# Reordering the query units of a fused four-layer kernel, and joining two heads' score tiles

## The chip, the cores and the metric

The kernel runs on one core of one Trainium2 chip. It is one program with one launch; the metric is the time of the program in microseconds (us), the median of several executions. Its engines are TensorE (PE, with its weight loads as PEld), VectorE (DVE), ScalarE (ACT), GpSimd (POOL) and SyncE (SP), which issues the DMAs. Each engine works through its own instructions in the order in which the program gives them, and waits at semaphores for the others.

## The reference

Input x has 2048 tokens of 128 features. Four layers follow each other, each an attention and a feed-forward part, both on a layer norm of the stream, in float32:

```python
x = x + L0_attn(layernorm(x))   # 16 heads of 8, full softmax over 2048 keys
x = x + L0_ffn(layernorm(x))    # 128 -> 512 -> 128, exact gelu
x = x + L1_attn(layernorm(x))   # 16 heads of 64, full softmax over 2048 keys
x = x + L1_ffn(layernorm(x))    # gated, integer weights / 127
x = x + L2_attn(layernorm(x))   # 16 heads of 8, each token sees its two neighbours, i-1 and i+1 modulo 2048
x = x + L2_ffn(layernorm(x))    # 8 experts, top 1
x = x + L3_attn(layernorm(x))   # a recurrence: 32 chunks of 64 tokens, each needs the state after the chunk before
x = x + L3_ffn(layernorm(x))    # 8 experts, top 2, and a shared one
```

Two things in it matter here. The second layer's attention (L1) is the bulk of the work. And in the third layer's attention (L2), token 0 needs token 2047: so the first block of the layers behind L1 attention needs the last token's L1 output, and each block needs the first token of the next.

## The kernel before

The stream stays on chip as `xs`, 128 x 16 x 128. The program has three stages. **The first** is layer 0, with the keys and values of layer 1 as they become ready; they go to DRAM (`kvd`, `khd`). **The second** is L1 attention (`l1_attn`, line 1066). **The third**, called the tail here, is what is left of the layers behind it, after the last score.

L1 attention runs over 40 *units*. A unit is one query block times one pair of heads (`units`, line 373). The five blocks stand in `QB` (line 33) as first token, number of tokens, and columns computed: 512, 384, 512, 384 and 256 tokens. The second block has 388 columns: its 384 own tokens and places for the *edge tokens* 1280, 1792 and 2047 (`EXTRA`), whose L1 output is computed early so that the neighbour attention of the layer behind needn't wait for their blocks. `stage_m` takes these few tokens alone through the L1 feed-forward part and makes the neighbours' keys and values; nothing of the neighbour attention starts before it (`s_b`, line 1959).

A unit has 16 *steps*, one for each 128 keys. In a step, for both heads of the pair:

- PE makes the scores, transposed (keys in the partitions), in four passes into two banks of the three in the pool `st`: high by high part, low by high, high by low, and the row of negated maxima (`ops`).
- ACT takes the exponentials into `P`, one tile of 128 x 512 for each head, from a pool of seven.
- PE makes a share of the *maxima products* for a later unit (`u_max`, `max_upto`): queries by keys into a bank of the pool `mx`, which DVE reduces to a row maximum (`mx<-mi` in the profile). The pool `mx` has five banks; the accumulator of the values and all banks of the other work come from it too.
- The tile of the step before is multiplied with the values (`do_pv`) and added to the sum of exponentials (`do_sum`, line 1099): by POOL into `acg` at steps 0 to 13, by DVE into `acd` at steps 14 and 15 (`dve` in `T`). The first tile of each sum is only noted, so POOL has 13 additions a head and DVE one; at the unit's end DVE adds `acg` to `acd` (`do_merge`).

`u_end` then makes the column sums, their reciprocals by way of DRAM, and the product `o<-o,rb` on DVE; `stage_wo` projects and adds to `xs`.

**What sets the order.** All instructions are put in order by hand in Python: the functions of all layers behind attention are generators in `parts` and `helpers`, and a planner with a clock for each engine (`note`, `clk`, `COST`) steps whichever piece is ready by its estimate. `fill` (line 246) is called between the exponentials and the products with the values; it steps pieces until PE's estimated clock has moved on by a limit. With `only="t"` it takes pieces alone that need no new bank and hold no product (`Part.may`, line 202). `fill` never changes what a piece does, only where it stands in each engine's queue.

Behind attention, blocks of 256 tokens go through `stage_a` and `stage_a2` (L1 feed-forward, and keys and values of the neighbours), `stage_b`, `stage_b2` (neighbour attention, top-1 experts), `stage_c` (inputs of the recurrence, 128 tokens at a time), `chunk` (32 of them in a chain), `stage_d`, `stage_g` (router of the last layer), `stage_e0` (starts the bank `ac` that sums the experts' outputs) and `s_lane`: 13 tiles of expert weights a block, spread over two lanes, and over seven in the tail, loaded from DRAM. In the built program the first block's `stage_e0` stands in unit 38, and no expert product before the tail.

Of the kernel before, what the change touches and what calls it, by code (L numbers as in the profile page):

```python
# [20 lines left out]
D = 128  # L21
# [10 lines left out]
T = dict(lead0=22, more0=4, mgap=0.4, pvq=2, lim0=0.5, fq=(3,), pl=-0.5, pr=1.0, tlow=2, tback=3, late=0.3, pvp="mx", mxp="mx", ex=(1280, 1792, 2047), low=1, lows='ge', keep=1, leave=2, pvn=1, sp=0, rdy=40., eu=2, qg=(22, 16, 10), em=2, el=6, sem=0.2, same=1.2, tsame=3.0, order="hdmBbAaEcCeg", ps=dict(st=3, mx=5), dma=2.3, slack=0.1, lim=0.3, backlog=2.5, lead=(10, 8, 6), pp=7, dve=(14, 15), qp=(1, 1), lanes=2, xl=5,  # L32
         QB=[(0, 512, 512), (512, 384, 388), (896, 512, 512), (1408, 384, 384), (1792, 256, 256)])

# [36 lines left out]
def body(ctx: ExitStack, tc: tile.TileContext, x, pa, pb, pc, pi, pd, pr, pr0, pe, pw, out):  # L71
# [90 lines left out]
    pp = ctx.enter_context(tc.tile_pool(name="pp", bufs=T["pp"]))  # L162
# [31 lines left out]
    class Part:  # L194
# [24 lines left out]
        def step(self):  # L219
            piece[0] = clk["T"]  # L220
            r = next(self.gen, "end")
            self.same = r == "same"
            self.ready = 0.0 if self.same else piece[0] + (r if type(r) is float else 0.0)
            self.pe = r == "T"
            self.banks = r if type(r) is int else 0
            self.seen = len(emitted) if r is False else -1
            if r == "end":
                emitted.add(self.key)
            return r != "end"
# [140 lines left out]

    QB = T["QB"]
    EXTRA = T['ex']
    units = [(qb, p) for qb in range(len(QB)) for p in range(NP1)]
    qhh, qfs, kmx, mx1 = {}, {}, {}, {}

    qx = [mid.tile([128, 8], F32R, name=f"qx{i}") for i in range(2)]
    xq = {}

    def u_loadx(qb):
        t0, tn, n = QB[qb]  # L380
        xq[qb] = l1x.tile([128, 512], F32, name="xq", tag="xq", bufs=2)
        if n != tn:
            ge.memset(xq[qb][:, tn:n], 0.0)
            for i, t in enumerate(EXTRA):
                sy.dma_start(xq[qb][:, tn + i:tn + i + 1], xnd[:, t:t + 1])
        sy.dma_start(xq[qb][:, :tn], xnd[:, t0:t0 + tn])

    def u_qprep(u):
        qb, p = units[u]
        if qb not in xq:  # L390
            u_loadx(qb)
# [3 lines left out]
        mm(ps[:, :n], C("wq", p * 128, 128), xq[qb][:, :n])  # L395
# [10 lines left out]
        if n > tn:  # L406
            for e in range(2):
                r = slice(64 * e, 64 * e + 64)
                se.copy(qx[u % 2][r, 4 * e:4 * e + n - tn], qf[r, tn:n])
# [15 lines left out]
    def u_max(u, i):  # L425
# [8 lines left out]
        if 128 * qt == tn:  # L434
            ps = amx()
            mm(ps[0:8], qx[u % 2], kmx[(u, c)])
            ve.tensor_reduce(mx1[u][0:8, 0, 3, c:c + 1], ps[0:8], AX.X, ALU.max)
# [11 lines left out]
    def u_maxend(u):  # L449
# [6 lines left out]
        if n > tn:  # L456
            ve.tensor_reduce(m[0:8, 0, 3:4], mx[0:8, 0, 3, :], AX.X, ALU.max)
        yield 1
        t = mi()
        if n > tn:  # L460
            te.transpose(t[0:1, 256:264], m[0:8, 0, 3:4], ident[0:8, 0:8])
# [5 lines left out]
        if n > tn:  # L467
            for e in range(2):
                se.mul(mbt[u % 2][64 * e:64 * e + 1, tn:n], t[0:1, 256 + 4 * e:256 + 4 * e + n - tn], -1.0)
# [50 lines left out]
    l0w = l0ctx.enter_context(tc.tile_pool(name="l0w", bufs=2))  # L520
    qd = dram.tile([16, 6, 8, S], BF16, name="qd")
# [150 lines left out]
    def l0_attn():  # L672
# [49 lines left out]
        for g in range(N):  # L722
# [9 lines left out]
            for q in range(4):  # L732
# [17 lines left out]
                p = pp.tile([128, 512], F32, name="P", tag="P")  # L750
# [202 lines left out]
    leave[0] = T["leave"]  # L953
# [10 lines left out]
    l1a = ctx.enter_context(tc.tile_pool(name="l1a", bufs=2, reuse_waits="tile"))  # L964
# [11 lines left out]
    def u_end(u, o, accs):  # L976
# [4 lines left out]
        if u == len(units) - 1:  # L981
            for e in range(2):
                mm(t[64 * e:64 * e + 64, :n], ones[:, 0:64], accs[e][:, :n], par=(e == 1))
# [8 lines left out]
        for e in range(2):  # L992
            mm(t[32 * e:32 * e + 32, :n], ones[:, 0:32], accs[e][:, :n], tile_position=(0, 32 * e), par=(e == 1))
# [29 lines left out]
    def stage_wo(qb, part):  # L1023
# [4 lines left out]
        for p in range(2 * part, 2 * part + 2):  # L1028
            mm(ps[:, :n], C("wo", p * 128, 128), O.pop(p)[:, :n], start=(p % 2 == 0), stop=(p % 2 == 1))
            yield  # L1030
        if part == 0:
            w = l1w.tile([128, 512], F32, name="wac", tag="wac", bufs=1)
# [9 lines left out]
        del wacc[qb]  # L1042
        yield 1
# [9 lines left out]
        if n != tn:  # L1053
            ne = len(EXTRA)
            xm = edge_x[0] = sm.tile([ne, 128], F32, name="xm", tag="xm", bufs=1)
            for i, t in enumerate(EXTRA):
                sy.dma_start(xm[i:i + 1, :], xs[t % 128:t % 128 + 1, t // 128, :])
# [8 lines left out]
    def l1_attn():  # L1066
        LEAD = dict(zip((256, 384, 512), T["lead"]))
        LEAD.update({260: LEAD[384], 388: LEAD[512]})
# [13 lines left out]
        def do_pv(g, pts, v):  # L1082
            u, k = divmod(g, 16)
            n = QB[units[u][0]][2]
            if k == 0:
                pv[u] = take([T["pvp"]])
            for e in range(2):
                mm(pv[u][64 * e:64 * e + 64, :n], v[:, k % SPC, 64 * e:64 * e + 64], pts[e][:, :n],
                   start=(k == 0), stop=(k == 15), par=(e == 1))
            if k == 15:  # L1090
# [5 lines left out]
                rel(pv.pop(u))  # L1096
                ends.append((u, o, accs))

        def do_sum(g, pts, v):
            u, k = divmod(g, 16)  # L1100
            n = QB[units[u][0]][2]
            for e in range(2):
                a = acc.setdefault(u, [None, None])
                f = first.setdefault((u, e), {})
                eng, nm = (ve, "d") if k in T["dve"] else (ge, "g")
                if nm not in f:
                    f[nm] = [pts[e]]
                    continue
                if len(f[nm]) == 1:
                    if u:  # L1110
                        need(("s", u - 1), ("o", u - 1))
                    t = l1a.tile([128, 512], F32, name="ac" + nm, tag="ac" + nm)
                    eng.tensor_tensor(t[:, :n], f[nm][0][:, :n], pts[e][:, :n], ALU.add)
                    f[nm] = [t, 1]
                else:
                    t = f[nm][0]
                    eng.tensor_tensor(t[:, :n], t[:, :n], pts[e][:, :n], ALU.add)
                if k == 15:
                    a[e] = f["d"][0]
                    merge.append((f["d"][0], f["g"][0], n))  # L1120
                    del first[(u, e)]
# [3 lines left out]
        def do_merge():  # L1125
            while merge:
                d, g_, n = merge.pop(0)
                ve.tensor_tensor(d[:, :n], d[:, :n], g_[:, :n], ALU.add)
            while ends:
                u, o, accs = ends.pop(0)  # L1130
                helper(("o", u), u_end(u, o, accs), max(wr[tname(t)] for t in accs))
# [4 lines left out]
        for g in range(16 * U):  # L1136
# [6 lines left out]
            if u + 2 < U:  # L1143
                if k == 1 and units[u + 2][1] == 0:
                    need(("q", u + 1))
                    u_loadx(units[u + 2][0])
# [10 lines left out]
            pts = []  # L1157
# [3 lines left out]
            for i, (a, b) in enumerate(ops):  # L1161
                for e in range(2):
                    rows = slice(64 * e, 64 * e + 64)
                    mm(pss[e][:, :n], a[rows], b[rows, :n], start=(i == 0), stop=(i == 3), par=e and 0.02)
            for e in range(2):
                pt = pp.tile([128, 512], F32, name="P", tag="P")
                se.activation(pt[:, :n], pss[e][:, :n], AF.Exp)
                rel(pss[e])
                pts.append(pt)
            max_upto(max_at(g + 16 + LEAD[n] + 1))  # L1170
            fill()
            if prev:
                do_sum(*prev[-1])
            if len(prev) == T["pvn"]:
                while prev:
                    do_pv(*prev.pop(0))
                fill()
            do_merge()
# [135 lines left out]
    def stage_m():  # L1314
# [22 lines left out]
        xt = sm.tile([128, 4], F32, name="xtm", tag="xtm", bufs=2)  # L1337
        yield from norm_T(xt)
        h = sm.tile([128, 12], F32, name="hm", tag="hm", bufs=1)
        for k in range(3):  # L1340
# [4 lines left out]
            th = sm.tile([128, 4], F32, name="thm", tag="thm", bufs=2)  # L1345
# [3 lines left out]
            ve.scalar_tensor_tensor(h[:, 4 * k:4 * k + ne], th[:, :ne], 0.5, ps[:, 64:64 + ne], ALU.mult, ALU.mult)  # L1349
# [3 lines left out]
        for k in range(3):  # L1353
            mm(ps[:ne, :128], h[:, 4 * k:4 * k + ne], tok(wi, 6 + k), start=(k == 0), stop=(k == 2))
# [763 lines left out]
```

## Time and profile before

| | |
|---|---|
| median of 3 runs | 2989.47 us (2988.46 to 3006.5) |
| the profiled execution | 3001.08 us, span 2999.2 us |
| first layer, to the first score of L1 | 0 to 906 us |
| L1 attention | 906 to 2596 us |
| tail | 2596 to 2999 us |
| PE / DVE / ACT / POOL busy | 2769.9 / 2194.9 / 1582.9 / 1522.3 us |
| POOL's additions `acg<-acg,P`, 960 of them | 1011.4 us, 1083 ns each |
| DVE's reductions `mx<-mi`, 2080 of them | 1322.1 us, 683 ns each |

A line of the table by stretches has the stretch, its length, the busy time and the number of instructions of PE, PEld (its weight loads), DVE, ACT and POOL, the granted share of PE's clock, the share of the DMA engines and GB/s. A wait line has who waited for whom, the total in us, the number of times, and the longest. A line of the timeline has start and duration in us, engine, line, operation, output and input tile, and shape. Nearly all instructions show one source line, 147, that of the helper through which they are issued; the tiles' names tell them apart. PE's records are modelled at their ends, so a busy PE includes some overlap.

### The profile page before, as it was taken

Reading aid. Unit: us, or ns where it says so; the run is one execution under the profiler, and the core shown is the slowest. Engines: PE = TensorE matmul, PEld = TensorE weight load, DVE = VectorE, ACT = ScalarE, POOL = GpSimd, SP = SyncE. Lnnn points to the kernel's source line nnn. Section 1 sums busy time; section 2 is a strip of 40 time slices with the busy share of each in tenths; the row PEclk is TensorE's granted clock in tenths of the full one; section 3 lists DMA queues with packets and bytes.
Section 4 is the critical chain, followed back from the end, with each engine's and each line's share of the span. In section 5 each row is a group of like instructions: output and inputs, shape, how many; then the busy total and the mean of one; then the engine's idle time right before and its main releaser. Section 6 shows DMA issues by size and latency. Waiting matters only on the chain.

```text
span 2999.2 us, 49776 instructions
## 1 busy us (share of the span) xinstructions
PE 2769.9 (92%) x16719; PEld 1307.0 (44%) x16719; DVE 2194.9 (73%) x4699; ACT 1582.9 (53%) x3933; POOL 1522.3 (51%) x1762
## 2 busy tenths in 40 slices
PE   7999999999979899999999999899989898888998
PEld 2222222322234344454444444455544555565666
DVE  7899898898534666566666778887677769787765
ACT  1788887888854444444444444444434334333444
POOL 2400110201127688866776876677767556443444
PEclk9999999999979999999999999999999999776779
DMA  6311231321144333433442332233334343312244
GB/s 142 72 28 22 72 84 17 101 54 46 53 141 135 92 112 110 121 110 111 138 119 87 94 95 87 89 105 108 109 97 114 108 117 94 88 52 61 76 104 115
DMA packets 247749, 275.80 MB, mean 92 GB/s; under 512 B 95747, under 2 KB 183330, under 8 KB 247366
## 3 DMA queue, kind: packets, MB, share of 16 engines
q1 hardware_dynamic: 246630, 272.43, 33.2%
q8 instruction: 132, 2.16, 0.3%
q14 instruction: 123, 1.01, 0.1%
q10 hardware_dynamic: 864, 0.20, 0.0%
HBM read 229.97 MB, written 42.28 MB: 91 GB/s over the span
## 4 chain that ended last, share of the span: by engine, by line
PE 70%; DVE 18%; ACT 6%; issue 3%; DMA 3%; POOL 1%; SPq 0%; ACTq 0%; DVEq 0%; POOLq 0%
PE mi L147 70%; DVE mx L147 5%; ACT P L147 3%; DVE sB L147 1%; DVE o L147 1%; DVE gq L147 1%; DMA ka<-kvd 1%; DVE gt L147 1%; DVE xs L147 1%; ACT kf L147 1%; ACT kh L147 1%; DVE xn L147 1%; DVE sG L147 1%; DVE acd L147 1%; DVE sA L147 0%
## 5 line engine op out<-in xcount | busy, mean ns | idle before, releaser
L147 DVE TENSOR_REDUCE mx<-mi 128x1 f32<-128x512 f32 (+1 forms) x2080 | 1322.1, 683 | 582.8 <-PE mi L147 571.5
L147 ACT ACTIVATE P<-mi 128x512 f32<-128x512 f32 (+3 forms) x2304 | 1137.0, 551 | 1004.1 <-PE mi L147 973.2
L147 POOL TENSOR_TENSOR acg<-acg,P 128x512 f32<-128x512 f32 (+3 forms) x960 | 1011.4, 1083 | 181.8 <-ACT P L147 180.0
L147 PE MATMUL mi<-P,ka 128*64 128x512 f32 (+3 forms) x2560 | 597.6, 546 | 2.3 <-DVE mx L147 2.3
L147 PE MATMUL mi<-qh,ka 64*128 64x512 f32 (+3 forms) x2560 | 521.0, 406 | 9.7 <-DMA ka<-kvd 6.8
L147 PEld LDWEIGHTS mi<-qh,ka 64*128 64x128 f32 x2560 | 247.0, 189 | 382.5 <-issue 347.0
L147 PE MATMUL mi<-kop,qop 48*128 48x512 bf16 x1024 | 348.6, 405 | 24.5 <-DVE mx L147 12.1
L147 PE MATMUL mi<-qop,kop 50*128 50x512 bf16 x1024 | 317.8, 391 | 27.1 <-ACT P L147 24.7
L147 PE MATMUL mi<-P,vop 128*32 128x512 f32 x2048 | 304.3, 623 | 13.9 <-ACT P L147 13.9
L147 POOL TENSOR_SCALAR vep<-mv 128x2 f32<-128x2 f32 (+1 forms) x24 | 5.5, 229 | 495.6 <-DVE mv L147 495.6
L147 PE MATMUL mi<-km,qh 64*128 64x512 f32 x1024 | 225.6, 410 | 30.4 <-DVE mx L147 23.8
L147 PE MATMUL mi<-mbt,onr 64*128 64x512 f32 (+3 forms) x1280 | 228.7, 351 | 1.5 <-DMA mbt<-mb 1.5
L147 PE MATMUL mi<-ql,ka 64*128 64x512 f32 (+3 forms) x1280 | 229.2, 353 | 0.0
L147 PEld LDWEIGHTS mi<-P,ka 128*64 128x64 f32 x2560 | 129.2, 137 | 225.3 <-issue 195.1
L147 PEld LDWEIGHTS <-kop 50*128 50x128 bf16 x1024 | 63.6, 95 | 304.9 <-issue 281.6
L147 POOL TENSOR_TENSOR acg<-P 128x512 f32<-128x512 f32 (+3 forms) x80 | 91.1, 1158 | 202.5 <-DVE acd L147 162.0
L147 PEld LDWEIGHTS mi<-km,qh 64*128 64x128 f32 x1024 | 107.1, 189 | 60.5 <-DVE mx L147 38.5
L147 PEld LDWEIGHTS mi<-mbt,onr 64*128 64x128 f32 x1280 | 124.6, 190 | 13.9 <-DMA mbt<-mb 2.2
L147 PEld LDWEIGHTS mi<-ql,ka 64*128 64x128 f32 x1280 | 125.7, 192 | 0.0
L147 PEld LDWEIGHTS <-qop 48*128 48x128 bf16 x1024 | 72.9, 96 | 97.2 <-issue 82.7
L147 PEld LDWEIGHTS mi<-P,vop 128*32 128x32 f32 x2048 | 55.5, 109 | 119.8 <-issue 90.7
L147 POOL TENSOR_TENSOR kl<-kf,kh 128x512 f32<-128x512 f32 x32 | 40.9, 1278 | 110.9 <-ACT kh L147 82.4
(509 smaller groups left out, 3464.4 us busy)
## 6 DMA issues: line engine op xcount, KB each, us to landing
ka<-kvd SPq DMA_DIRECT2D x320, 384.0 KB
km<-khd SPq DMA_DIRECT2D x159, 256.0 KB
khd<-kh SPq DMA_DIRECT2D x32, 256.0 KB
kvd<-kh SPq DMA_DIRECT2D x32, 256.0 KB
kvd<-kl SPq DMA_DIRECT2D x32, 256.0 KB
kvd<-vt SPq DMA_DIRECT2D x16, 512.0 KB
ka<-in_pw_dram SPq DMA_DIRECT2D x37, 192.0 KB
w3s<-in_pw_dram SPq DMA_DIRECT2D x35, 192.0 KB
```

What stands on the lines that cost most here:

```text
L147: r = f(*a, **k)
```

## The change

1. The edge tokens move to the first block, and there are five of them: 256, 768, 1280, 1792 and 2047, one at each start of a later block. The first block shrinks to 384 tokens in 392 columns, and the second grows to 512.
2. The units run in another order: two units of block 1, all eight of block 0, the other six of block 1, then blocks 2, 3 and 4. (The two units whose maxima are made during the first layer are then 512 wide, as before.)
3. Both heads' exponentials go into one tile, `P` of 128 x 2 x 512, from a pool of five that lives in attention and the tail alone. The sums are one instruction for both heads: 1024 columns in place of two of 512. DVE takes the steps 5, 6, 11 and 12, POOL the other twelve.
4. `fill(9.0, "t")` is also called after the first, second and third score pass, and at three places after the exponentials: pieces without a product and without a new bank enter there. The pieces that hold a product are marked as such (`yield "T"`) where they weren't.
5. `stage_e0` waits for the tail (`fa=0`); the branch with `own`, in which an expert tile has its own bank, is then not used.
6. While no accumulator of values is held, pieces behind attention leave one more bank free (`leave`).

The planner's estimates of costs are as before.

```diff
-T = dict(... ex=(1280, 1792, 2047), ... pp=7, dve=(14, 15), ...
-         QB=[(0, 512, 512), (512, 384, 388), (896, 512, 512), (1408, 384, 384), (1792, 256, 256)])
+T = dict(pp1=5, fa=0, ti=(0, 1, 2), tf=1, ... ex=(256, 768, 1280, 1792, 2047), ... pp=7, dve=(5, 6, 11, 12), ...
+         QB=[(0, 384, 392), (384, 512, 512), (896, 512, 512), (1408, 384, 384), (1792, 256, 256)])
...
-            self.pe = r == "T"
+            self.pe = r == "T" or type(r) is float
...
-    units = [(qb, p) for qb in range(len(QB)) for p in range(NP1)]
+    SEG = [(1, 0, 2), (0, 0, 8), (1, 2, 8), (2, 0, 8), (3, 0, 8), (4, 0, 8)]
+    units = [(qb, p) for qb, p0, p1 in SEG for p in range(p0, p1)]
...
-            mm(ps[0:8], qx[u % 2], kmx[(u, c)])
-            ve.tensor_reduce(mx1[u][0:8, 0, 3, c:c + 1], ps[0:8], AX.X, ALU.max)
+            mm(ps[0:2 * NX], qx[u % 2], kmx[(u, c)])
+            ve.tensor_reduce(mx1[u][0:2 * NX, 0, 3, c:c + 1], ps[0:2 * NX], AX.X, ALU.max)
...
-    l1a = ctx.enter_context(tc.tile_pool(name="l1a", bufs=2, reuse_waits="tile"))
+    l1a = ctx.enter_context(tc.tile_pool(name="l1a", bufs=1, reuse_waits="tile"))
+    pp = ctx.enter_context(tc.tile_pool(name="pp", bufs=T["pp1"], reuse_waits="tile"))
...
         def do_sum(g, pts, v):
             u, k = divmod(g, 16)
             n = QB[units[u][0]][2]
-            for e in range(2):
-                a = acc.setdefault(u, [None, None])
-                f = first.setdefault((u, e), {})
-                eng, nm = (ve, "d") if k in T["dve"] else (ge, "g")
-                if nm not in f:
-                    f[nm] = [pts[e]]
-                    continue
...
-                    t = f[nm][0]
-                    eng.tensor_tensor(t[:, :n], t[:, :n], pts[e][:, :n], ALU.add)
...
+            f = first.setdefault(u, {})
+            eng, nm = (ve, "d") if k in T["dve"] else (ge, "g")
+            if nm not in f:
+                f[nm] = [pts]
+            elif len(f[nm]) == 1:
...
+                t = l1a.tile([128, 2, 512], F32, name="ac" + nm, tag="ac" + nm)
+                eng.tensor_tensor(t[:, :, :n], f[nm][0][:, :, :n], pts[:, :, :n], ALU.add)
+                f[nm] = [t, 1]
+            else:
+                t = f[nm][0]
+                eng.tensor_tensor(t[:, :, :n], t[:, :, :n], pts[:, :, :n], ALU.add)
+            if k == 15:
+                acc[u] = f["d"][0]
+                merge.append((f["d"][0], f["g"][0], n))
...
                     mm(pss[e][:, :n], a[rows], b[rows, :n], start=(i == 0), stop=(i == 3), par=e and 0.02)
+                if T["tf"] and i in T["ti"]:
+                    fill(9.0, "t")
+            pts = pp.tile([128, 2, 512], F32, name="P", tag="P")
             for e in range(2):
-                pt = pp.tile([128, 512], F32, name="P", tag="P")
-                se.activation(pt[:, :n], pss[e][:, :n], AF.Exp)
+                se.activation(pts[:, e, :n], pss[e][:, :n], AF.Exp)
                 rel(pss[e])
-                pts.append(pt)
             max_upto(max_at(g + 16 + LEAD[n] + 1))
             fill()
+            if T["tf"]:
+                fill(9.0, "t")
...
     def s_e0():
         for b in range(NB_):
             yield from wait(("g", b))
-            if b and not tail:
-                yield from wait(("l", b - 1))
+            while not tail and b >= T["fa"]:
+                yield False
             yield from mark(("e0", b), stage_e0(b))
```

## The prediction

> **What bounds the kernel now.** I read the page's busy shares, then its 40 slices, then the same table over stages chosen by me: query blocks of the second layer's attention from 906 to 2596 us (40 units of 16 steps; a unit is one head pair of one query block), then a tail of experts and recurrence.
>
> ```profile
> PE 2769.9 (92%) x16719; PEld 1307.0 (44%) x16719; DVE 2194.9 (73%) x4699; ACT 1582.9 (53%) x3933; POOL 1522.3 (51%) x1762
> ...
> PEclk9999999999979999999999999999999999776779
> ```
>
> ```profile
> 906.00:2596.00 1690.00, 1609.63 (x10123) 795.71 (x10123) 1187.42 (x2335) 750.20 (x1934) 1203.47 (x1269) 0.97 0.37 107
> 2596.00:2999.00 403.00, 343.46 (x1715) 256.06 (x1713) 288.45 (x1065) 159.70 (x658) 167.20 (x279) 0.76 0.31 79
> 1040.00:1500.00 460.00, 456.38 (x2820) 215.19 (x2816) 287.08 (x498) 221.31 (x489) 350.86 (x317) 1.00 0.39 117
> 1540.00:2280.00 740.00, 704.84 (x4224) 342.26 (x4220) 554.51 (x1077) 323.26 (x816) 525.42 (x523) 0.97 0.33 98
> 2280.00:2596.00 316.00, 285.96 (x2136) 164.23 (x2135) 245.47 (x615) 126.15 (x476) 191.63 (x292) 0.91 0.42 110
> ```
>
> The columns are length, then busy us of PE, PEld, DVE, ACT and POOL, then the granted clock. Attention is PE's: 1040 to 1500 is full at clock 1.00. Later it isn't: PE's busy time times the clock is 684 of 740 us (8% lost) and 260 of 316 (18% lost). In the tail it is 261 of 403: 142 us are lost, to waits and a low clock. I then asked what PE waits for in attention, and looked into the longest of these waits.
>
> ```profile
> PE mi L147 <- DVE mx L147: 36.2, 25, 6.6
> PE mi L147 <- DVE m L147: 17.3, 5, 8.9
> ```
>
> ```profile
> 971.82 10.90 DVE L147 TENSOR_TENSOR o<-o,rb 128x512 f32<-128x512 f32 x1
> ```
>
> ```profile
> 967.38 14.79 POOL L147 TENSOR_TENSOR acg<-acg,P 128x512 f32<-128x512 f32 x12
> ```
>
> A DVE product of two SBUF tiles, 0.68 us when quick, stood 10.9 us under POOL's unbroken row of additions; behind it waited the maxima, and PE stood idle for 8.9 us. At 2178 us `u` stood 8.0 us and PE 6.6; at 1569 us `o` 5.9 and PE 4.6. Sixteen such cases (over 1.5 us above the form's quick ones) hold 61 us of DVE, and 36 us of PE's idle time lie within 3 us of them.
>
> **The change, part by part.**
>
> *Units in another order.* With all edge tokens in the block that is finished second, the layer behind attention starts at unit 10 instead of 16. In the two built programs the tail falls from 914 PE instructions to 730, and from 18 recurrence chunks to 10; all 208 expert first products stay in it in both. The 184 that leave are mostly chunk products, which follow each other at 0.22 us (2617.73, 2617.95, 2618.18 in the timeline): 40 us of PE, added to attention, where PE is full.
>
> *The tail.* It is split at its last chunk (2925 us). Before it 735 PE instructions took 329 us, 0.448 each; after it 179 took 74, 0.413 each. The new program has 471 and 259: 211 + 107 = 318 us. Bounds: if only the chunk chain counts (17.1 us from chunk to chunk between 2617.7 and 2908.3), 9 x 17.1 + 21 before + 16 after + 107 = 298; if the loss of 142 us stays whole and only 40 us of work goes, 363. The first expert block's accumulation and its lane loads used to be issued in unit 38; now they follow the last score, so the first experts wait for a load: nothing if chunks cover it, 5.9 us by the chain's longest load piece there (`km<-rwd`). I take 318 + 6 = 324, that is **-79 us**, with -40 and -99 as ends.
>
> *Both heads' tiles side by side.* POOL's addition costs 1.311 us at 512 columns and 0.738 at 256, so 0.165 fixed and 2.24 ns a column; 1024 columns are then 2.46 us. A 512-wide unit goes from 26 additions of one head (34.1 us) to 11 of both (27.0). Before, POOL needs 2.62 us in each of 14 steps of 2.52 (unit time 40.3 us over 16), so it falls behind and leaves no gap; after, 2.46, and at most four steps in a row, with two steps' rest. Over all units 220 us of 1102 go. The starvation should shrink: 36 us of PE idle, and the half-clock windows after it. In all of attention 80 us of PE idle stand beside 116 us at half clock, so each idle us costs 0.72 more: 62 us to be had at most. But one addition now blocks for 2.46 us instead of 1.31. I take half, **-31**; the ends are 0 and -62.
>
> The Trainium skill, "SBUF — State Buffer", section "Who interferes with whom", says that a DVE instruction with two SBUF inputs and a GpSimd instruction reading SBUF exclude each other for a whole instruction. That speaks against doubling the instruction: by it alone the blocked instruction's longest single wait rises by 1.15 us and nothing is gained; the trace's 10.9 us under nine additions says that the row of them is the larger part.
>
> *Sums moved to DVE.* It gets 3 double additions and one double merge a unit, in place of 2 and 2 single ones. Single costs 0.684 us at 512 columns and 0.405 at 256, so a double one 1.24 and 0.69: +2.2 us a 512-wide unit, +1.7 a 384-wide, +1.1 a 256-wide; 16, 16 and 8 of them: 71 us. The tail's 300 fewer DVE instructions (1036 to 736), at 288.45/1065 = 0.27 us, bring 81 more. DVE goes from 1187 of 1690 (70%) to about 1339 of 1730 (77%). What is queued behind each on DVE is the reductions that free the banks PE's maxima need. If waits grow as load over slack, 0.77/0.23 against 0.70/0.30 is 1.43: on 53.5 us of waits for DVE, +23, and with the clock's 0.72, +40. On the 17.5 us that aren't starvation it is +13. Nothing and +94 (a rival below) are the ends; I take **+36**. The merge now follows POOL's own last addition (step 15, before step 13): DVE may stand there up to 2.46 us a unit; it stands behind the next step's scores and maxima, some 2.5 us later, so I add nothing beyond that range.
>
> *Pieces between score passes.* They hold no PE instruction; they only stand earlier in the queues of ACT, DVE and POOL, before the exponentials instead of after. ACT is 44% busy in attention and PE waits 3.8 us for `P` in all. If a piece is late, the exponential behind it holds one of three score banks; a piece emitted in time shortens a hop by up to a step. No row separates the two: -4 (that wait gone) to +8 (tripled), I take 0. *Larger edge tile, pools:* five single-column loads for three, twice 16 rows for 8: 32 `qx` maxima at the same 0.68 us; nothing. Five double P tiles for seven single ones are ten heads' worth; nothing.
>
> **Sum.** +40 - 79 - 31 + 36 = -34 us. The profiled execution took 3001.1 us (span 2999.2), 11.6 above the median 2989.5; it would become 2967, the median **2955**.
>
> The Trainium skill, "TensorE: Matmul & The Clock Gate", section "What's actually happening", gives half clock after an idle window of about 3.4 us. Between 2750 and 2800 us PE was busy 47.1 of 50 us at clock 0.56, so here it comes also without such a gap. By the rule a denser tail would run at full clock (261 - 40 + 56 idle, about 280); the rows say otherwise, and I keep them.
>
> **Rivals.** One per cent, 30 us, is about what a measurement here can tell from no change.
> 1. *DVE becomes the bound* (slower). Longer POOL holds and 7 points more load put the stretch 1540 to 2280 where 2280 to 2596 is now, with DVE at 78% and 18% lost: 684/0.82 = 834, +94 us. In place of +36: 3013; with the starvation unrelieved too (+31), 3044. It decides from a loss of 12.5% there, 2 us a unit over those 16 units. For it: every long PE wait in attention names DVE. Against: POOL loses 220 us, and DVE's wait with it. Chance 0.24 for over 3019.
> 2. *The tail only sheds its work* (no difference). Experts and clock bound it, not chunks: 363 us, -40, eaten by the +40 in attention; with -31 and +36, 2995. For it: 142 us of loss can't all be the chain's. Against: 0.448 us an instruction with chunks for products averaging 0.29. Chance 0.28 for 2960 to 3019.
> 3. *Starvation gone and tail at the chain's pace*: -62 +20 +40 -99 = -101, 2888. Chance 0.12 for under 2925.
> My forecast, 2925 to 2960, has 0.36. So faster by over 1% 0.48, within 0.28, slower 0.24. The range leaves a tenth on each side: 2905 to 3035.
>
> **What would show it.** Tail of 300 to 350 us, 10 chunks in it, PE's clock still near 0.75. Attention 1715 to 1755 us, POOL about 985 us busy, DVE about 1340, no DVE instruction over 6 us, PE's waits for `mx` and `m` under 60 us. If DVE passes 80% there and `mx` waits double, rival 1 holds; if the tail is over 355, rival 2. I'd be wrong outright if an engine other than these held PE, ACT by late pieces above all.

## The result, and the profile after

The changed kernel takes 3011.2 us in the median (2996.0 to 3020.3), the kernel before 2996.9 (2981.3 to 3012.1): ratio 1.0050, 95% interval 1.0035 to 1.0066. It is slower by half a per cent, 15 us; 34 us faster was forecast. The time lies inside the range, and within the one per cent called no change, but the sign is wrong, and it is clear of noise.

The page of the changed kernel, engines and clock:

```profile
PE 2763.8 (92%) x16719; PEld 1296.0 (43%) x16719; DVE 2353.3 (78%) x4702; ACT 1596.9 (53%) x3938; POOL 1326.4 (44%) x1159
...
PEclk9999999999979999999999999999999999978879
```

The same stretches as before, for the changed kernel: attention, the tail, then units 10 to 15, 16 to 23, 24 to 31 and 32 to 39 (length; busy us of PE, PEld, DVE, ACT, POOL; granted clock):

```profile
902.00:2695.00 1793.00, 1684.64 (x10445) 836.85 (x10443) 1414.21 (x2652) 787.19 (x2115) 1028.45 (x720) 0.96 0.34 101
2695.00:3009.00 314.00, 266.64 (x1394) 203.69 (x1392) 220.79 (x750) 137.42 (x482) 146.54 (x225) 0.84 0.38 102
1276.00:1574.00 298.00, 285.70 (x1560) 128.50 (x1556) 253.95 (x412) 133.24 (x299) 175.69 (x91) 0.99 0.31 92
1574.00:2024.00 450.00, 419.66 (x2254) 193.99 (x2252) 385.48 (x697) 188.63 (x466) 254.35 (x163) 0.95 0.28 82
2024.00:2388.00 364.00, 336.93 (x2150) 176.08 (x2148) 295.25 (x575) 154.09 (x432) 201.11 (x154) 0.95 0.34 99
2388.00:2695.00 307.00, 279.82 (x2187) 163.61 (x2183) 231.53 (x609) 131.20 (x512) 156.32 (x177) 0.93 0.39 109
```

The tail gave 89 us (403 to 314), as hoped. Attention took 103 (1690 to 1793). Some 43 of these are products that moved into it: every product counted with its spacing at full clock gives 1546 us before and 1589 after. The other 60 are what PE loses beside its products, which the forecast had at +5. PE's idle time rose by 28 us (80 to 108 by the rows above and in the prediction), some 17 of them waits for DVE and 11 for DMAs; the time at half clock rose from 116 to 145 us, which costs some 14; the rest, some 18, lies within what the profile counts as busy PE and is not broken down here. POOL is busy for 175 us less there (1203 to 1028), DVE for 227 more (1187 to 1414), of which the forecast had 152. What PE waits for in attention now:

```profile
PE mi L147 <- DVE mx L147: 52.1, 44, 3.2
PE mi L147 <- DVE m L147: 2.7, 5, 0.9
```

The long waits for these two are gone (longest 8.9 us before, 3.2 now), but there are many more short ones: 44 for `mx` in place of 25. Their sum hardly moved, 53.5 us before and 54.8 now; what rose are waits for other DVE results (`h`, `dz` and the like, most of them of the layers behind attention). One of the short waits, in DVE's timeline at 1871 us, then POOL's, then PE's:

```profile
1870.41 1.29 DVE L147 TENSOR_REDUCE mx<-mi 128x1 f32<-128x512 f32 x2
1871.62 3.30 DVE L147 TENSOR_TENSOR acd<-P 128x1024 f32<-128x1024 f32 x1
1874.84 2.83 DVE L147 TENSOR_TENSOR o<-o,rb 128x512 f32<-128x512 f32 x1
1877.59 2.47 DVE L147 TENSOR_REDUCE mx<-mi 128x1 f32<-128x512 f32 x4
```

```profile
1871.46 8.42 POOL L147 TENSOR_TENSOR acg<-acg,P 128x1024 f32<-128x1024 f32 x3 [13.03 <-ACT P L147]
```

```profile
1878.32 0.79 PE L147 MATMUL mi<-km,qh 64*128 64x512 f32 x1 [3.24 <-DVE mx L147]
```

Two DVE instructions in a row, each with two inputs in SBUF, stand behind POOL's additions. DVE's own sum, 1.21 us when quick, takes 3.30; `o`, 0.68 when quick, takes 2.83. In 6 us of DVE's queue 1.9 us of work is done, four reductions come late, and PE stands for 3.2 us. By form, POOL's additions and DVE's sums in attention (mean ns after the busy time):

```profile
L147 POOL TENSOR_TENSOR acg<-acg,P 128x1024 f32<-128x1024 f32 x160 | 397.6, 2485 | 251.0 <-ACT P L147 234.1 <-ACT dz L147 3.6 <-ACT thm L147 2.5
```

```profile
L147 DVE TENSOR_TENSOR acd<-acd,P 128x1024 f32<-128x1024 f32 x32 | 59.2, 1849 | 0.0
L147 DVE TENSOR_TENSOR acd<-P 128x1024 f32<-128x1024 f32 x16 | 47.4, 2962 | 0.0
```

POOL's addition costs the 2.46 us that were forecast. DVE's sums were priced at 1.24 us, and the first of each unit costs 2.96 in the 512-wide ones, since POOL's last addition before DVE's turn is still running: in 14 of these 16 units one was under way when DVE's sum started. Before the change DVE's sums stood at the unit's end and cost 0.683 us each, undisturbed:

```profile
L147 DVE TENSOR_TENSOR acd<-P 128x512 f32<-128x512 f32 x32 | 20.6, 683 | 0.0
```

### The profile page after: what moved, and what is told of

Its sections match the earlier page's. It is cut to its first block, busy times and chain, and to the rows that moved or that the text cites. A ratio compares the mean times of both kernels' runs of the same rounds, so it can differ in the third digit from the quotient of the medians.

```text
span 3009.0 us, 48067 instructions
## 1 busy us (share of the span) xinstructions
PE 2763.8 (92%) x16719; PEld 1296.0 (43%) x16719; DVE 2353.3 (78%) x4702; ACT 1596.9 (53%) x3938; POOL 1326.4 (44%) x1159
## 5 line engine op out<-in xcount | busy, mean ns | idle before, releaser
L147 POOL TENSOR_TENSOR acg<-acg,P 128x1024 f32<-128x1024 f32 (+3 forms) x400 | 814.9, 2037 | 527.1 <-ACT P L147 475.3
L147 PE MATMUL mi<-P,ka 128*64 128x512 f32 (+3 forms) x2560 | 605.6, 553 | 1.0 <-DVE xs L147 0.7
L147 PE MATMUL mi<-qh,ka 64*128 64x512 f32 (+3 forms) x2560 | 527.9, 409 | 15.8 <-DMA ka<-kvd 13.2
L147 PE MATMUL mi<-km,qh 64*128 64x512 f32 x1024 | 239.6, 415 | 35.8 <-DVE mx L147 26.5
L147 POOL TENSOR_TENSOR acg<-P 128x1024 f32<-128x1024 f32 (+3 forms) x40 | 82.5, 2062 | 96.4 <-DVE acd L147 46.0
L147 DVE TENSOR_TENSOR acd<-acd,P 128x1024 f32<-128x1024 f32 (+3 forms) x80 | 113.1, 1414 | 0.2
```

The source lines that it names most:

```text
L147: r = f(*a, **k)
```

## The experiments

Three theories were set against each other. HOLD: POOL's addition keeps DVE's instructions with two SBUF inputs out while it runs, and the doubled one does so for longer. LOAD: DVE has too much to do, however long POOL's instructions are (one half of the prediction's first rival; the other half is longer holds). FILL: the pieces between the score passes stand too early and hold up the exponentials.

In the table "held" is DVE's time in attention above its quick forms, reductions left out: for each form (operation, tiles, shape) the quickest twentieth over all runs is taken as its price, and what lies above it is summed, for the sums `acd` and for all others. Ratios are to the kernel before, run beside each. "Over 3 us" counts the DVE instructions in attention that stand more than 3 us over their quick form. Attention, tail, POOL's busy share of attention and the held times are from the profiled run, the tail to its last product. Two profiled runs lie more than 10 us off their median: with DVE's sums cut it is 17 us over it, with POOL's sums cut in the kernel before 18 under. The kernel before took 2997 us beside the changed kernel and 3000 to 3005 beside the others, so a time of theirs is up to 8 us high against an expectation reckoned from 2997; the ratios are free of that. A kernel with sums cut computes less than the reference and serves as a measurement only.

| kernel | ratio (95%) | attention | tail | POOL busy | held: sums + others | over 3 us |
|---|---|---|---|---|---|---|
| before | 1 | 1688 | 402 | 71% | 4 + 194 us | 8 |
| changed | 1.0050 (1.0035 to 1.0066) | 1793 | 311 | 57% | 79 + 226 | 0 |
| order alone | 1.0086 (1.0047 to 1.0126) | 1765 | 362 | 68% | 2 + 229 | 12 |
| tiles alone | 1.0063 (1.0038 to 1.0089) | 1724 | 392 | 59% | 81 + 221 | 1 |
| no fill | 1.0129 (1.0100 to 1.0159) | 1760 | 373 | 58% | 72 + 223 | 0 |
| POOL in halves | 0.9917 (0.9886 to 0.9948) | 1759 | 310 | 63% | 26 + 194 | 10 |
| POOL in quarters | 0.9929 (0.9895 to 0.9962) | 1773 | 311 | 71% | 18 + 180 | 12 |
| POOL and DVE in halves | 0.9989 (0.9963 to 1.0014) | 1782 | 318 | 62% | 86 + 178 | 9 |
| halves, DVE at the end | 1.0057 (1.0032 to 1.0083) | 1809 | 296 | 68% | 2 + 266 | 12 |
| joined, DVE 6 steps | 0.9941 (0.9914 to 0.9968) | 1778 | 310 | 50% | 99 + 181 | 0 |
| halves, DVE 6 steps | 0.9724 (0.9685 to 0.9762) | 1701 | 321 | 58% | 35 + 156 | 1 |
| halves, DVE 8 steps | 0.9707 (0.9667 to 0.9748) | 1682 | 330 | 50% | 47 + 108 | 0 |
| DVE's sums cut | 0.9912 (0.9882 to 0.9942) | 1769 | 318 | 56% | 87 + 219 | 0 |
| POOL's sums cut | 0.9505 (0.9472 to 0.9539) | 1642 | 312 | 18% | 2 + 54 | 0 |
| before, POOL's sums cut | 0.9702 (0.9655 to 0.9748) | 1598 | 390 | 25% | 4 + 26 | 0 |
| order, POOL's sums cut | 0.9602 (0.9563 to 0.9641) | 1617 | 357 | 24% | 2 + 23 | 0 |
| before, DVE's steps spread | 0.9985 (0.9963 to 1.0006) | 1698 | 401 | 64% | 85 + 149 | 3 |

### The parts of the change one by one

The order alone:

```diff
-T = dict(... tf=1, ... dve=(5, 6, 11, 12), ...
+T = dict(... tf=0, ... dve=(14, 15), ...
...
-                eng.tensor_tensor(t[:, :, :n], t[:, :, :n], pts[:, :, :n], ALU.add)
+                for e in range(2):
+                    eng.tensor_tensor(t[:, e, :n], t[:, e, :n], pts[:, e, :n], ALU.add)
```

> The unit order and edge tokens alone: no pieces between score passes, sums of each head by themselves, DVE at steps 14 and 15 as before (P stays a double tile, from five). 15 chunks are left in the tail, before 18, after the whole change 10. Theory HOLD (the doubled POOL addition blocks DVE for 2.4 us at a time, and that ate the gain): faster than before, 2970 to 2985 us, tail about 375, attention about 1700, DVE's time above its quick forms near the 195 us of before. Theory LOAD (DVE has too much to do, whatever the length of POOL's instructions): 2980 to 2995, as the moved chunks load DVE too. Theory FILL (pieces between the passes stand too early): 2970 to 2985.

It is slower, by 0.9%. The tail fell by 40 us, but attention rose by 77, with only 16 us of products moved into it. The DVE instructions that stand over 3 us went from 8 to 12, the longest takes 11.0 us again. What PE waits for there:

```profile
PE mi L147 <- DVE mx L147: 41.5, 28, 6.8
PE mi L147 <- DVE dz L147: 12.1, 3, 5.9
PE mi L147 <- DVE xs L147: 10.2, 3, 4.5
```

All three theories had it under 2996, so none foresaw this. The moved chunk and block work runs on DVE in a stage where POOL keeps DVE out; the cut below tells whether that is the cause.

The joined tiles alone:

```diff
-T = dict(... tf=1, ... ex=(256, 768, 1280, 1792, 2047), ...
-         QB=[(0, 384, 392), (384, 512, 512), ...
+T = dict(... tf=0, ... ex=(1280, 1792, 2047), ...
+         QB=[(0, 512, 512), (512, 384, 388), ...
...
-    SEG = [(1, 0, 2), (0, 0, 8), (1, 2, 8), (2, 0, 8), (3, 0, 8), (4, 0, 8)]
+    SEG = [(0, 0, 8), (1, 0, 8), (2, 0, 8), (3, 0, 8), (4, 0, 8)]
```

> The joined tiles and DVE's steps 5, 6, 11 and 12 alone, with the old blocks, edge tokens and unit order and no pieces between score passes; 18 chunks in the tail as before. HOLD: slower than before, 3010 to 3040 us, all of it in attention, with many PE waits of 2 to 3 us for DVE's maxima. LOAD: 71 us more of sums on DVE, 3005 to 3015. FILL: 2985 to 3000, since POOL's long rows are gone and nothing else is added.

Slower by 0.6%, 36 us more in attention, as HOLD has it (3024 us, for 3010 to 3040); FILL's 2985 to 3000 fails. LOAD's 3005 to 3015 does not fall here: counted from 2997 the time is 3016, and the interval reaches down to 3008. So this run does not tell HOLD from LOAD. POOL's busy time fell, and DVE's held time rose from 198 to 302 us.

Without the pieces between the passes:

```diff
-T = dict(... tf=1, ...
+T = dict(... tf=0, ...
```

> The whole change without pieces between the score passes; 16 chunks in the tail. HOLD: attention 1690 + 10 of moved work + 30 to 40 of waits, tail 385: 3010 to 3030 us. LOAD: 3000 to 3015. FILL: 2960 to 2985, faster than the change and than before.

FILL falls: without the pieces the kernel is slower, 1.0129 against 1.0050, and slower than any of the theories had it. Nor does PE wait longer for the exponentials with them, 2.4 us in all for `P` in the changed kernel and 3.8 before:

```profile
PE mi L147 <- ACT P L147: 2.4, 4, 0.9
```

They bring six chunks out of the tail (16 without them, 10 with): the tail is 62 us longer without them, attention 33 shorter.

### How long one POOL addition holds

From here on the instructions of the changed kernel stay in their places, where nothing else is said: the planner is told of one whole addition, and only what is issued differs.

```diff
+        def add(eng, o, a, b):
+            if eng is ge:
+                for e in range(2):
+                    eng.e.tensor_tensor(o[:, e], a[:, e], b[:, e], ALU.add)
+            else:
+                eng.e.tensor_tensor(o, a, b, ALU.add)
+            note(eng.n, "tensor_tensor", (o, a, b, ALU.add), {})
...
-                eng.tensor_tensor(t[:, :, :n], t[:, :, :n], pts[:, :, :n], ALU.add)
+                add(eng, t[:, :, :n], t[:, :, :n], pts[:, :, :n])
```

> The changed kernel with every POOL addition issued as two, one for each head; every other instruction in the same place. POOL gets some 73 us more to do (440 times 0.165), DVE the same. HOLD: faster than the changed kernel by 20 to 40 us, 2970 to 2990, with DVE's time above its quick forms down from 287 us to about 200 in attention. LOAD and FILL: 3005 to 3025, not faster than the changed kernel.

```profile
L1112 POOL TENSOR_TENSOR acg<-acg,P 128x512 f32<-128x512 f32 x320 | 435.5, 1388 | 196.6 <-ACT P L147 196.3
```

```profile
902.00:2662.00 1760.00, 1666.38 (x10449) 830.92 (x10447) 1332.97 (x2651) 787.35 (x2117) 1116.79 (x1159) 0.96 0.37 103
```

HOLD holds: POOL is busy for 88 us more, DVE for 81 us less, attention is 34 us shorter, and the kernel is faster than both, at 0.9917. In the program nothing changed but that each of POOL's additions became two of half the length. Ten DVE instructions stand over 3 us again, where the joined additions left none, and yet the held time falls from 305 to 220 us: many holds of some 2 us cost more than these ten.

In quarters:

```diff
+                w = o.shape[2] // 2
+                for e in range(2):
+                    for c in (slice(0, w), slice(w, 2 * w)):
+                        eng.e.tensor_tensor(o[:, e, c], a[:, e, c], b[:, e, c], ALU.add)
```

> The changed kernel in the same order, with every POOL addition issued as four, each of half a head's columns. The hold is 0.74 us at 512 columns in place of 2.4, but four take 2.95 us a step of 2.5, so POOL's unbroken rows return. HOLD by the length of one instruction: at or under the time with halves, 2960 to 2980. HOLD by the unbroken row: back up, 2985 to 3020, with single waits of over 5 us. LOAD: 3005 to 3030.

At 2990 us it lies where the unbroken row was expected to put it, but by the ratios it is not to be told from the halves. The held time of the sums falls further (18 us), but POOL is busy for 71% of attention again, and 12 DVE instructions stand for over 3 us longer than their quick forms, up to 6.8 us in all. Below half the length nothing more is gained; that the unbroken row is what takes the gain back fits these numbers, but no run shows it by itself.

DVE's sums in halves as well:

```diff
+            for e in range(2):
+                eng.e.tensor_tensor(o[:, e], a[:, e], b[:, e], ALU.add)
```

> The changed kernel in the same order with POOL's and DVE's additions and the merge issued as one for each head. Against POOL's halves alone (2978 us) it tells whether DVE's own doubled additions matter, which POOL and the maxima wait for: HOLD says little, 2970 to 2990; if the joined DVE instruction matters as POOL's does, 2955 to 2968.

Worse than POOL's halves alone (0.9989 against 0.9917), which neither case expected. The held time of the sums goes back to 86 us: of the 120 sums 25 stood in both halves and 59 in at least one (over 0.3 us above the quick form), where 33 of the 120 joined ones stood. On the side that waits, joining helps; on the side that holds, it hurts.

POOL in halves, DVE's turn at the end as before the change (the planner's own order, 8 chunks in the tail):

```diff
-T = dict(... dve=(5, 6, 11, 12), ...
+T = dict(... dve=(14, 15), ...
```

> The changed kernel with POOL's additions as halves, and DVE's steps 14 and 15 as before the change (13 additions on POOL, one on DVE and the merge); the planner's order is its own, with 8 chunks in the tail instead of 10. DVE has 71 us less to do than with halves alone, POOL gets the row of 14 steps back. LOAD: faster than with halves, 2945 to 2970. HOLD by the unbroken row: slower than with halves, 2980 to 3010.

Slower than the halves alone by 1.4%, though DVE has less to add: LOAD fails again, and HOLD's 2980 to 3010 is exceeded too. POOL's row of 14 steps is back, and with it DVE instructions of up to 7.6 us. The two chunks that moved into attention (25 us more of PE's busy time there, 14 us less of tail) are a part of the difference that this run does not separate.

### What POOL's hold costs in all

POOL's additions but each unit's first are cut to 4 columns a head, so these sums are left out:

```diff
+            c = 4 if eng is ge and tname(o) == tname(a) else o.shape[2]
+            eng.e.tensor_tensor(o[:, :, :c], a[:, :, :c], b[:, :, :c], ALU.add)
```

> The changed kernel in the same order, with 10 of POOL's 11 additions a unit cut to 4 columns a head (these sums are left out; each unit's first addition is whole). It takes POOL's hold away nearly whole, and leaves DVE's own work. HOLD: attention falls from 1793 to 1700 to 1730, DVE's time above its quick forms from 287 us to under 120, total 2935 to 2965. LOAD: attention loses under 20 us, total 2990 to 3010, since DVE still has its sums and chunks.

```profile
903.00:2545.00 1642.00, 1611.71 (x10443) 809.00 (x10444) 1173.64 (x2649) 785.85 (x2116) 302.89 (x720) 0.99 0.40 110
2545.00:2858.00 313.00, 268.02 (x1400) 204.37 (x1398) 220.62 (x754) 138.41 (x484) 146.65 (x226) 0.84 0.39 102
```

```profile
PE mi L147 <- DMA ka<-kvd: 16.7, 13, 3.1
PE mi L147 <- DMA xq<-xnd: 4.3, 1, 4.3
PE mi L147 <- DVE mx L147: 3.5, 3, 2.2
```

More than HOLD expected: attention is 151 us shorter, and 53 us of it remain above its products (1642 against 1589). DVE still makes all its own sums, chunks and blocks, but takes 1174 us for them instead of 1414, and PE's waits for `mx` fall from 52.1 to 3.5 us. The tail stays as it was, 313.

The same for DVE's later sums and the merge (left out):

```diff
+            c = 4 if eng is ve and tname(o) == tname(a) else o.shape[2]
```

> The changed kernel in the same order, with DVE's second and third addition and its merge cut to 4 columns a head in each unit (left out of the sums), some 110 us of DVE's busy time away. POOL's doubled additions stay. LOAD: attention falls by 40 to 60 us, total 2950 to 2975. HOLD: by 10 to 25, total 2985 to 3005, since the long waits of all other DVE instructions stay.

Here LOAD comes closer. In microseconds 2981 lies between LOAD's 2975 and HOLD's 2985; counted from 2997 it is 2971, inside LOAD's range. The 24 us of attention in the table would be HOLD's figure, but the profiled execution took 2998 us, the most of its eight. By the ratios (1.0050 to 0.9912) the cut is worth 1.4%, 41 us, for 96 us less on DVE. So the load counts too, about a quarter as much as POOL's additions (1.0050 to 0.9505, 163 us). DVE's sums, cut as they are, still stand behind POOL: 87 us held.

The same cut in the kernel before, and in the order alone (24 of 26 additions a unit to 8 or 4 columns, left out of the sums, order as in those kernels):

```diff
+                    c = 8 if eng is ge else n
+                    eng.e.tensor_tensor(t[:, :c], t[:, :c], pts[e][:, :c], ALU.add)
+                    note(eng.n, "tensor_tensor", (t[:, :n], t[:, :n], pts[e][:, :n], ALU.add), {})
```

> The kernel before, in its own order, with 24 of POOL's 26 additions a unit cut to 8 columns (these sums are left out). It prices POOL's hold in the kernel before, as the same cut priced it in the changed one (152 us of 3011). HOLD with the length of one instruction as what the change made worse: the price before is clearly smaller, 70 to 110 us, total 2885 to 2930. If the price is the same 150 us, total about 2850, the change made nothing worse there and the loss lies elsewhere.

> The unit order alone, with POOL's additions after each unit's first cut to 4 columns (these sums are left out), same order as that run (3032 us). HOLD: the order alone lost by POOL's hold falling on more moved work in attention, so the cut is worth more than the 88 us that it was before the change: 110 to 150 us, total 2880 to 2920, below the kernel before with the same cut (2916). If the cut is worth 88 us again, about 2943, the order itself loses by something else.

Both times lie in HOLD's ranges, and together they price the hold. In per cent of the kernel before (30 us each), it costs 3.0 in the kernel before (1 to 0.9702), 4.8 with the order alone (1.0086 to 0.9602), and 5.5 in the changed kernel (1.0050 to 0.9505). Without POOL's sums the order gains 1.0 (0.9702 to 0.9602), and the whole change 2.0 (to 0.9505), 59 us. The hold grew by 2.5, 74 us. 74 less 59 is the 15 us lost; that this comes out even is arithmetic, since both are made of the same four ratios. Each of these differences is uncertain by about 0.4 to 0.7 by the intervals in the table. So the growth with the order alone, 1.8, is clear of noise, and the 0.6 from there to the whole change is not: there the broken rows, the longer instruction and the further chunks that moved in come together. One limit: the cut takes the additions away, and with them whatever else waits for them, so it prices POOL's additions as a whole; that the length of one of them is a part of the price is shown by the halves.

### Row, length and load

The kernel before, with DVE's steps spread and one addition a head:

```diff
-T = dict(... dve=(14, 15), ...
+T = dict(... dve=(5, 6, 11, 12), ...
```

> The kernel before with DVE's steps 5, 6, 11 and 12 in place of 14 and 15, single tiles and one addition a head as before. POOL's row of 14 steps is broken up without doubling its instruction; beside the run with joined tiles alone (3024 us) it tells row from length. HOLD: faster than before, 2975 to 2995, no DVE instruction over 8 us, DVE's time above its quick forms under 180 us. LOAD: 71 us more on DVE, 3005 to 3015.

No difference, 0.9985. LOAD's 3005 to 3015 fails. HOLD's range is met only as counted from 2997 (2992 us), and its held time of under 180 us is not: it is 234. The row is broken up (3 instructions over 3 us for 8, the others' held time down from 194 to 149), but DVE's sums, now beside POOL's, are held for 85 us in place of 4. Against the joined tiles alone, 1.0063, it shows the length's price in the old order.

The changed kernel with six steps for DVE, first with POOL's additions in halves, then with them joined:

```diff
-T = dict(... dve=(5, 6, 11, 12), ...
+T = dict(... dve=(3, 4, 7, 8, 11, 12), ...
```

> POOL's additions as halves, and DVE at six steps (3, 4, 7, 8, 11, 12) in place of four, so POOL has 9 double additions a unit for 11 and rests after every two steps; order by the planner, 10 chunks in the tail. HOLD: POOL's time falls by a fifth, and with it DVE's waits: 2950 to 2970, the fastest. LOAD: DVE gets 2 x 1.2 us a unit more, about 80 us: 2985 to 3010.

> The changed kernel with DVE at steps 3, 4, 7, 8, 11 and 12, and POOL's additions whole again (2.4 us each). Against the same with halves (2921 us) it tells the length of one instruction from its share of the time. HOLD by the length: clearly slower than with halves, 2945 to 2975. HOLD by POOL's share of the time alone: within 10 us of it, 2915 to 2932. LOAD: slower than the changed kernel, over 3011.

Attention, with POOL in halves and then joined:

```profile
902.00:2603.00 1701.00, 1643.84 (x10444) 824.39 (x10445) 1372.72 (x2729) 788.97 (x2116) 987.45 (x998) 0.98 0.38 106
```

```profile
904.00:2682.00 1778.00, 1680.28 (x10448) 834.96 (x10447) 1459.81 (x2729) 788.68 (x2116) 895.33 (x640) 0.96 0.35 102
```

With halves this is 2.8% faster than the kernel before, 2921 us and under HOLD's range; joined, 2987, above it. POOL is busy for 92 us *more* than with joined additions, and attention is 77 us shorter: the length weighs more here than POOL's share of the time. The share is not nothing: at the same length, DVE's six steps in place of four leave POOL 9 additions a unit for 11 and shorter rows, and gain 1.1% joined (1.0050 to 0.9941) and 1.9% in halves (0.9917 to 0.9724). LOAD as the bound falls for this range: DVE does more sums than in the changed kernel and is 81% busy (1373 of 1701), in place of 79%, at 92 us less.

Eight steps:

```diff
-T = dict(... dve=(5, 6, 11, 12), ...
+T = dict(... dve=(2, 3, 6, 7, 10, 11, 13, 14), ...
```

> POOL's additions as halves, DVE at eight steps (2, 3, 6, 7, 10, 11, 13, 14), POOL at the other eight; the planner leaves 12 chunks in the tail. It looks for the point from which DVE's load decides: HOLD alone would give another 20 to 30 us, 2890 to 2905; if the load of another 2.4 us a unit decides, 2925 to 2960.

0.9707, not to be told from six steps. The held time falls to 155 us, attention by 19 more, but two chunks fall back into the tail. It lies between the two expectations, so the point from which DVE's load decides wasn't reached clearly. These two beat both kernels; the best median of a kernel that makes all sums is 2914 us.

## Why the prediction was wrong, step by step

- **What bounds the kernel, and by what it loses: right.** DVE behind POOL's additions was named from the trace, and the cut shows it as the largest loss of attention in either kernel, 89 us before. The prediction had "62 us to be had at most" there.
- **The tail: right, -89 for -79.** Its last chunk is at 2888 us, 121 before the end, where 107 were forecast; before it 193 us in place of 211. The two parts missed by 14 and 18 us in opposite directions, so that the sum fits so well is in part luck. The PE clock rose to 0.84, where 0.75 was expected. (In the sum that ends at about 280 the tail's idle time, 56 us, is 60 by its own row; nothing rests on it.)
- **What moves the chunks: wrong in attribution.** The prediction gave all eight to the order of the units and put the pieces between passes at 0. In the built programs of the experiments the order takes 3 of the 18 (2 with joined tiles), and the pieces 6 more; without the pieces the kernel is 0.8% slower.
- **The moved products: right,** +43 for +40. **POOL's addition: right,** 2.485 us for 2.46.
- **The starvation: the step that failed.** "I take half, -31", with ends of 0 and -62, took DVE's standing behind POOL to shrink. It grew: by the cuts POOL's additions cost 89 us before and 163 after, 74 us more (2.5%, uncertain by 0.6). The long rows did go: no DVE instruction now stands 3 us over its quick form, where 8 did. But 76 now stand 1.5 us or more over theirs, where 17 did (16 by the prediction's own measure), up to 2.7 us each, and held time went from 198 to 305 us. The runs show two reasons that the bounds left out.
  - *The longer hold.* With POOL's additions in halves and everything else in the same place the kernel is 1.3% faster (1.0050 to 0.9917), which turns the sign of the whole change. The Trainium skill's rule that the two engines exclude each other for a whole instruction, "SBUF — State Buffer", section "Who interferes with whom", was weighed and set aside there; the halves say that it should have carried the sign.
  - *The moved work.* The 40 us of PE and 81 us of DVE that move into attention were priced at what they take undisturbed. With the order alone, one-head additions and whole rows, the price of POOL's additions is already up from 3.0 to 4.8%, and the order, which was to bring the gain, loses 0.9%.
- **The sums on DVE: mis-sized.** They were priced as undisturbed, 71 us; beside POOL they are held for another 79. The forecast's +36 rested on load alone. The load does count, 41 us for 96 us less on DVE, but it is not the bound: at 81% and 83% busy the kernel is faster.
- **Rival 1 had the sign and not the mechanism.** It put the loss on DVE's load as the bound and on longer holds together. Its time did not come either (over 3019 us), and that its 3013 lies so near 3011 is luck. By the cuts POOL's additions cost four times what DVE's own later sums do; the stretch it named, units 16 to 31, is at 814 us for 740, where it had 834. Of these 74 us 28 are products that moved in (706 us at full-clock spacing for 677).
- **The signs.** The tail's 314 us, its 10 chunks, the longest DVE instruction (3.9 us) and PE's waits for `mx` and `m` (54.8 us, under 60) were as foreseen; attention (1793 us for 1715 to 1755), POOL (1028 for 985), DVE (1414 for 1340) and the tail's clock were not. That the waits for the maxima stayed put while attention grew by 103 us says that they were too narrow a sign: the hold reaches PE by other results of DVE as well.

## What to carry to other kernels

Where VectorE and GpSimd both work on SBUF, joining GpSimd's instructions to save their fixed cost can lose: one instruction's length is the time for which the other engine's two-input instructions stand, and here 1.3 to 2.2% of the kernel (40 to 65 us) hung on 2.5 us against 1.4. Keep the holder's instructions short, give it fewer of them where the waiting engine has room, and join those of the engine that waits. Work that is moved into a stage meets that stage's contention, so price it by what the same forms take there, not by their quick ones.

## What the runs showed of the hardware

- Bringing work forward into attention was worth 1.0% without POOL's additions and cost 0.9% with them: contention turned the sign of the same edit.
- A DVE addition split in two waited more than a joined one: 86 us held in place of 26, and 25 of 120 sums stood in both halves.
- Not only instructions with two tensors from SBUF stood behind POOL. In the changed kernel's attention TENSOR_SCALAR stood 49 us over its quick forms in all and COPY, with one input, 10; with POOL's sums cut it was 5 and under 1. No TENSOR_REDUCE stood more than 0.03 us over its quick form (1081 of them).
- With POOL's sums cut, attention in units 32 to 39 (256 columns) still took 292 us for products of 255, with waits for the key tiles (`ka<-kvd`, 16.7 us in all) and half clock; that loss has another cause, which no run here took up.
